# Two graph-attention layers and an FFN: layer 2's attention terms moved into the last head of layer 1, and three smaller moves

## The chip, the cores and the metric

The kernel runs on one core of a Trainium2 chip. The metric is device time in microseconds (us) of one execution. The engines named below are PE (TensorE, matrix products), DVE (VectorE), ACT (ScalarE), POOL (GpSimd) and SP (SyncE, which here issues nearly all DMAs). [...]

## The reference, cut to what matters

x has 1250 rows (nodes) of 768 values. With 21,250 edges (src, dst), the program computes

```python
def gat_layer(x, W, att_src, att_dst, bias, src, dst, heads, out_ch):
    h = (x @ W.T).reshape(n, heads, out_ch)
    a_src, a_dst = einsum('nhc,hc->nh', h, att_src), einsum('nhc,hc->nh', h, att_dst)
    e = leaky_relu(a_src[src] + a_dst[dst], 0.2)
    ex = exp(e - segment_max(e, dst)[dst])
    alpha = ex / (segment_sum(ex, dst)[dst] + 1e-16)
    return segment_sum(alpha[:, :, None] * h[src], dst) + bias

g = relu(gat_layer(layernorm(x), W1, ..., heads=8, out_ch=128))   # layer 1: 1250 x 1024
x = x + gat_layer(g, W2, ..., heads=1, out_ch=768)                # layer 2
x = x + ffn(layernorm(x))     # 768 -> 384 -> 768 with gelu; the first 6 rows take routed experts
```

## The kernel before, in words

The 1250 nodes are cut into 10 blocks of 125. A first stage counts the edges between every source and every destination node with one-hot products (to about 168 us); the counts (`ct`) then turn the sparse softmax into dense matrices. All sums are in float32.

**Layer 1** is a loop over eight heads `h` and ten source blocks `s` (from L740). For each, `weights` (L577) makes a tile `pt` of 125 sources by 1250 destinations in three steps: DVE adds and takes a maximum (L581), ACT takes Exp (L584), DVE limits and multiplies by the counts (L585). Three such tiles exist at a time. PE then multiplies the tile with the head's features, ten products of 129 columns (L749), into four accumulators `acc`. When a head is complete, `finish_head` (L654) runs inside the next head's step 0: DVE makes reciprocals (L661, L664), ACT rescales (`on`, L671), PE transposes (`h1tp`, L674), and ACT writes layer 1's output `g` with bias and relu (L675).

Other work is placed in the same loop. `top_of_block` (L555, its instruction at L557) takes, for one head and one source-side block, the row maximum over the neighbours, on DVE; the 120 of them that lie ahead of layer 2 are spread over the steps by hand (`top_steps`, L647). `load_destination_rows` (L562) prepares a head's two destination rows; its helper `rows_to_dram` (L518) transposes on PE, copies on DVE (L523) and sends the rows through DRAM, from where SP loads them broadcast to all partitions. `fold_att2` (L688, after heads 3 and 4) folds layer 2's attention vectors into W2, giving `v2` (1024 by 2): products on PE (L696), copies to `v_row` on DVE (L702), small transposes, copy to `v2`. `h2_part` (L722) makes one of the 20 pieces of the first half of layer 2's features `h2` (8 PE records each, L726); five pieces go into each of heads 4 to 7.

**The seam.** After head 7, `finish_head` runs once more, and layer 2's two attention terms are formed: `a2p` (L779 to L785) multiplies `v2` with `g`, head by head, in four column spans of 375, 375, 250 and 250 nodes. The four spans sit in four groups of PE's columns (32 each). DVE copies the result to `a2_row` (L787); the row goes to DRAM (`as2_d`), comes back broadcast, and DVE takes layer 2's ten tops. Meanwhile PE makes the second half of `h2` (another 20 pieces). Then come layer 2's weights (`weights2`, L823), its products (L905), a layer norm, and the FFN (`ffn_block`, L948), which stores each block with `store_rows` (L119).

**What sets the order.** A scheduler (the tile framework) decides the order on each engine when the program is built; it works from the order in which the kernel records operations and from its own costs. An edit in one place can thus move instructions elsewhere. Buffers come from pools: for PE's results there are six banks for products (`ps_mm`) and two for transposes (`ps_tr`).

Of the kernel before, what the change touches and what calls it, by code (L numbers as in the profile page):

```python
# [34 lines left out]
N = 1250  # L35
D = 768
E = 21250
H1, C1 = 8, 128
# [4 lines left out]
B = 125  # L43
NB = N // B
# [23 lines left out]
def gnn_ffn(  # L68
# [25 lines left out]
    nc = tc.nc  # L94
# [12 lines left out]
    def ps_mm(name):  # L107
        return mm_pool[0].tile([128, 512], F32, tag="mm", name=name)
# [266 lines left out]
    def act_copy(o, i):  # L375
        nc.scalar.activation(o, i, AF.Copy)  # L376
# [54 lines left out]
    groups, h1v = [], []  # L431
# [20 lines left out]
    for g in range(2):  # L452
        for h in range(H1):
            j = h % 4
            nc.tensor.matmul(
                vt[g][32 * j : 32 * j + 32, :384], att[:, h], w1n[h // 4][:, h % 4, g * 384 : (g + 1) * 384],
                start=(h < 4), stop=(h >= 4),
# [9 lines left out]
    p = ps_tr("vp")  # L467
    for k in range(KD):
        nc.tensor.matmul(
            p[:, 32 * k : 32 * k + 32], vt_s[:, k * 128 : (k + 1) * 128], pick_head,  # L470
            start=True, stop=True,
# [14 lines left out]
    spans = [(0, 3), (3, 6), (6, 8), (8, 10)]  # L486
    p = ps_mm("a1p")
# [30 lines left out]
    def rows_to_dram(cols, n, name, sp):  # L518

        p = ps_tr(f"{name}_p")  # L520
        nc.tensor.transpose(p[:n, :B], cols, ident[:B, :B])
        s = sp.tile([2 * NB, B], F32, tag="rowst", bufs=2, name=f"{name}_s")
        nc.vector.tensor_copy(s[:n], p[:n, :B])  # L523
        d = dram.tile([n, B], F32, name=f"{name}_d")
        nc.sync.dma_start(d, s[:n])
        return d
# [127 lines left out]
    def finish_head(h, acc):  # L654

        rec = ap.tile([B, NB], F32, tag="rec", bufs=2, name=f"rec{h}")
        avs = []
        for g in range(NG):
            n = min(PER, NB - g * PER)
            avs.append(acc[g][:B, : n * (C1 + 1)].rearrange("p (j c) -> p j c", j=n))  # L660
            nc.vector.tensor_scalar(  # L661
                rec[:, g * PER : g * PER + n], avs[g][:, :, C1], DEN_EPS, None, op0=OP.add
            )
        nc.vector.reciprocal(rec, rec)  # L664
        for g in range(NG):
            n = min(PER, NB - g * PER)
            av = avs[g]
            on = ap.tile([B, PER, C1], F32, tag="on", bufs=3, name=f"on{h}_{g}")
            for j in range(n):
                d = g * PER + j  # L670
                nc.scalar.activation(on[:, j], av[:, j, :C1], AF.Copy, scale=rec[:, d : d + 1])  # L671
            p = ps_tr(f"h1tp{h}_{g}")
            for j in range(n):
                nc.tensor.transpose(p[:, j * B : (j + 1) * B], on[:, j], ident[:B, :B])  # L674
            nc.scalar.activation(  # L675
                groups[h // 4][:, h % 4, g * PER * B : (g * PER + n) * B], p[:, : n * B],
                AF.Relu, bias=b1c[:, h : h + 1], scale=1.0,
            )
# [9 lines left out]
    def fold_att2(g):  # L688
        w2n = half_w(1, f"w2n{g}").rearrange("p (k f) -> p k f", k=KD)
        nc.sync.dma_start(  # L690
            w2n, w2[:, g * 512 : (g + 1) * 512].rearrange("(k p) f -> p k f", p=128)
        )
        p = ps_tr(f"v2p{g}")
        for k in range(KD):
            for j in range(2):
                nc.tensor.matmul(  # L696
                    p[32 * j : 32 * j + 2, :256], att2c[:, k], w2n[:, k, j * 256 : (j + 1) * 256],
                    start=(k == 0), stop=(k == KD - 1),
                )
        for j in range(2):  # L700
            c = g * 512 + j * 256
            nc.vector.tensor_copy(v2_row[:, c : c + 256], p[32 * j : 32 * j + 2, :256])  # L702
        p = ps_tr(f"v2tp{g}")
        for h in range(4 * g, 4 * g + 4):
            nc.tensor.transpose(
                p[:, 2 * h : 2 * h + 2], v2_row[:, h * C1 : (h + 1) * C1], ident[:2, :2]
            )
        nc.vector.tensor_copy(
            v2[:, 4 * g : 4 * g + 4],
            p[:, 8 * g : 8 * g + 8].rearrange("p (h t) -> p h t", h=4),  # L710
        )
# [10 lines left out]
    def h2_part(i, b, g):  # L722

        p = ps_mm(f"h2p{i}_{b}_{g}")
        for h in range(4):
            nc.tensor.matmul(  # L726
                p[:B, :384], groups[i][:, h, b * B : (b + 1) * B],
                w2h[i][:, h, g * 384 : (g + 1) * 384], start=(h == 0), stop=(h == 3),
            )
        o = h2[0][:, b, g * 384 : (g + 1) * 384]  # L730
        if i == 0:
            act_copy(o, p[:B, :384])
        else:
            nc.vector.tensor_add(o, p[:B, :384], o)

    h2_first = [(b, g) for b in range(NB) for g in range(2)]
    load_w2(0)
    todo = None
    for h in range(H1):
        hd = heads[h]  # L740
        acc = [ps_mm(f"acc{h}_{g}") for g in range(NG)]
        for s in range(NB):
            pt = ap.tile([B, N], F32, tag="pt", bufs=3, name=f"pt{h}_{s}")
            weights(pt, hd, as1_lo[:, h, s : s + 1], as1_hi[:, h, s : s + 1], s, 0, N)
            if s in top_steps.get(h, ()):
                tops.pop(0)()
            for d in range(NB):
                g, j = divmod(d, PER)
                nc.tensor.matmul(  # L749
                    acc[g][:B, j * (C1 + 1) : (j + 1) * (C1 + 1)],  # L750
                    pt[:, d * B : (d + 1) * B], h1v[h // 4][:, h % 4, s, :],
                    start=(s == 0 and j == 0), stop=(s == NB - 1), skip_group_check=True,
                )
            if s == 0 and todo is not None:
                finish_head(*todo)
            if s == 3 and h + 1 < H1:
                load_destination_rows(heads[h + 1], ap, a1[:, 1, h + 1], f"h{h + 1}", 2)
            if s == 0 and h == 3:
                load_source_row(heads[7], ap, as1_d[7], "h7")
            if h >= 4 and s in (2, 3, 5, 6, 8):  # L760
                h2_part(0, *h2_first.pop(0))
            if fill and s in (4, 7) and len(fill) > 2 * (3 - h) - (s == 7):
                fill.pop(0)()
        if h == 3:
            h2.append(big.tile([B, NB, D + 1], F32, tag="t", name="h2"))
            nc.gpsimd.memset(h2[0][:, :, D : D + 1], 1.0)
        if h in (3, 4):
            fold_att2(h - 3)
        if h == 5:
            load_w2(1)  # L770
        todo = h, acc
    finish_head(*todo)
    attn.close()


    second = ExitStack()
    sp = pool("second", stack=second)
    a2_row = sp.tile([2, N], F32, tag="src_row", bufs=1, name="a2_row")
    p = ps_mm("a2p")  # L779
    for h in range(H1):  # L780
        for j, (b0, b1) in enumerate(spans):
            nc.tensor.matmul(  # L782
                p[32 * j : 32 * j + 2, : (b1 - b0) * B], v2[:, h],
                groups[h // 4][:, h % 4, b0 * B : b1 * B], start=(h == 0), stop=(h == H1 - 1),
            )  # L785
    for j, (b0, b1) in enumerate(spans):
        nc.vector.tensor_copy(  # L787
            a2_row[:, b0 * B : b1 * B], p[32 * j : 32 * j + 2, : (b1 - b0) * B]
        )
    as2_d = dram.tile([1, N], F32, name="as2_d")  # L790
    nc.sync.dma_start(as2_d, a2_row[0:1])
    a2 = const.tile([B, NB, 2], F32, name="a2")
    p = ps_tr("a2tp")
# [154 lines left out]
    def ffn_block(q):  # L948

        gt = fp.tile([128, KH, 2, B], F32, tag="gt", bufs=2, name=f"gt{q}")  # L950
        for m in range(KH):
            p = ps_mm(f"f1_{q}_{m}")
            for k in range(KD):
                nc.tensor.matmul(  # L954
                    p[:, : 2 * B], wf1[:, k, m * 128 : (m + 1) * 128],
                    xt2[q][:, k].rearrange("p i j -> p (i j)"), start=(k == 0), stop=(k == KD - 1),
                )
            nc.scalar.activation(
                gt[:, m].rearrange("p i j -> p (i j)"), p[:, : 2 * B], AF.Gelu,
                bias=fc1c[:, m : m + 1], scale=1.0,  # L960
            )
        for i in range(2):
            d = 2 * q + i
            o = fp.tile([B, D], F32, tag="o", bufs=3, name=f"o{d}")
            nc.gpsimd.tensor_add(o, x2[d], fc2br)
            for g in range(2):
                p = ps_mm(f"f2_{d}_{g}")
                c = slice(g * 384, (g + 1) * 384)
                for m in range(KH):
                    nc.tensor.matmul(  # L970
                        p[:B, :384], gt[:, m, i, :], wf2[:, m, c],
                        start=(m == 0), stop=(m == KH - 1),
                    )
                nc.vector.tensor_add(o[:, c], p[:B, :384], o[:, c])  # L974

            r0 = NCLS if d == 0 else 0
            if d == 0:
                nc.sync.dma_start(out[r0:B], o[r0:])
            else:
                store_rows(out[d * B : (d + 1) * B], o)  # L980


# [161 lines left out]
```

## Time and profile before

| what | value |
|---|---|
| time, median of 3 runs | 787.17 us (786.72 to 787.53) |
| the profiled execution's own time | 786.1 us |
| its span, first to last instruction | 784.3 us |
| granted PE clock, mean | 0.991 of full speed |
| PE busy | 745.2 us (95%), 4612 instructions |
| DVE busy | 580.0 us (74%), 974 instructions |
| ACT busy | 323.7 us (41%), 589 instructions |
| POOL busy | 121.1 us (15%) |

Busy shares are means over stages with different limits. PE's ends are modelled from a pipeline, so that a busy PE can also be a PE that waits a little between two products; where exactness matters, starts of instructions are compared. In a row of instructions "x20" means 20 records; a float32 product of this kernel shows as two records, a transpose as one. The stages lie at: edge counts to 168 us, heads 0 to 3 from 200 to 338, heads 4 to 7 to 491, the seam to 503, the second half of `h2` to 553, layer 2 to 685, FFN to 784.

### The profile page before, as it was taken

The numbers are of one execution on the slowest core, as the hardware profiler recorded it, in microseconds if no ns is written. First come the engines' busy times: TensorE is split into PE (matmuls) and PEld (weight loads), VectorE is DVE, ScalarE is ACT, GpSimd is POOL, SyncE is SP. The second block draws the span as 40 slices with busy tenths as digits, with TensorE's granted clock in tenths as the row PEclk, the third lists the DMA queues.
The fourth block names the chain that finished last, engine by engine and source line by source line (L and its number), as shares of the span: only waits on it lengthen the run. The fifth ranks groups of instructions, "written<-read, shape, count | busy, mean of one in ns | idle before, by whom it ended". The sixth has DMA issues, their size and how long they took to land.

```text
span 784.3 us, 11527 instructions
## 1 busy us (share of the span) xinstructions
PE 745.2 (95%) x4612; PEld 493.4 (63%) x4612; DVE 580.0 (74%) x974; ACT 323.7 (41%) x589; POOL 121.1 (15%) x104
## 2 busy tenths in 40 slices
PE   4988998999989999899999999999999999999997
PEld 1553443544777777788888888455555555576755
DVE  7859999999999999999878785297856622251412
ACT  4989987522355546453635462202331300011000
POOL 5236677200000000000000000100010101023010
PEclk9999999899999999999999999999999999999999
DMA  9651000017002020422220100402211001094811
GB/s 238 217 207 41 3 1 1 2 67 242 37 2 67 1 67 1 147 81 67 81 67 1 67 1 2 152 0 69 64 36 31 29 20 40 0 316 111 329 40 40
DMA packets 21553, 58.49 MB, mean 75 GB/s; under 512 B 2385, under 2 KB 7627, under 8 KB 20344
## 3 DMA queue, kind: packets, MB, share of 16 engines
q1 hardware_dynamic: 21496, 57.72, 22.3%
q8 instruction: 37, 0.61, 0.3%
q14 instruction: 20, 0.16, 0.1%
HBM read 53.74 MB, written 3.98 MB: 74 GB/s over the span
## 4 chain that ended last, share of the span: by engine, by line
PE 60%; DVE 13%; issue 3%; ACT 2%; ACTq 0%; DVEq 0%
PE acc L905 15%; PE h2p L726 13%; PE acc L749 12%; DVE pt L581 6%; PE f L970 5%; PE f L954 5%; DVE pt L585 5%; PE h1p L443 4%; DVE unused L557 2%; PE h1tp L674 1%; ACT on L671 1%; PE a2p L782 1%; PE xt2p L372 1%; PE candp L1067 1%; PE v2p L696 1%
## 5 line engine op out<-in xcount | busy, mean ns | idle before, releaser
L584 ACT ACTIVATE pt<-pt,as_lo 125x1250 f32<-125x1250 f32 (+1 forms) x130 | 128.0, 1012 | 202.7 <-DVE pt L581 188.1
L749 PEld LDWEIGHTS acc<-g,pt 125*125 125x125 f32 x1600 | 185.0, 188 | 25.3 <-DVE pt L585 17.5
L749 PE MATMUL acc<-g,pt 125*125 125x129 f32 x1600 | 191.8, 275 | 7.1 <-DVE pt L585 7.1
L585 DVE SCALAR_TENSOR_TENSOR pt<-pt,ct 125x1250 f32<-125x1250 f32 (+1 forms) x130 | 133.2, 1053 | 11.9 <-ACT pt L584 11.5
L905 PE MATMUL acc<-h,pt 125*125 125x385 f32 (+1 forms) x400 | 129.7, 486 | 0.0
L581 DVE SCALAR_TENSOR_TENSOR pt<-rows_h,as_hi 125x1250 f32<-125x1250 f32 x80 | 119.8, 1514 | 11.0 <-PE acc L749 10.8
L443 PE MATMUL h1p<-w1s,xt 128*125 128x512 f32 x240 | 109.2, 597 | 0.6 <-ACT g L376 0.5
L905 PEld LDWEIGHTS acc<-h,pt 125*125 125x125 f32 x400 | 74.6, 187 | 53.9
L726 PE MATMUL h2p<-w2s,g 128*125 128x384 f32 x320 | 107.4, 487 | 0.0
L268 POOL TENSOR_SCALAR to<-node,dst_f 125x64 bf16<-125x64 f16 (+4 forms) x63 | 80.1, 1471 | 50.7 <-PE count L294 48.7
L726 PEld LDWEIGHTS h2p<-w2s,g 128*125 128x125 f32 x320 | 58.1, 187 | 37.7 <-issue 0.9
L294 PE MATMUL count<-ring,to 125*32 125x512 bf16 (+1 forms) x729 | 69.6, 362 | 6.4 <-DVE ring L219 5.3
L443 PEld LDWEIGHTS h1p<-w1s,xt 128*125 128x125 f32 x240 | 42.7, 188 | 47.4 <-issue 45.6
L294 PEld LDWEIGHTS <-to 125*32 125x32 bf16 x1068 | 37.7, 99 | 53.6 <-issue 23.8
L901 POOL TENSOR_TENSOR xb<-xb,b2r 125x768 f32<-125x768 f32 x10 | 18.5, 1850 | 326.0 <-DVE a_row L787 180.4
L219 DVE TENSOR_SCALAR ring<-node,src_f 125x1250 bf16<-125x1250 f16 x116 | 59.7, 545 | 7.0 <-PE count L294 4.5
L294 PE MATMUL count<-absent,to 125*32 125x512 bf16 (+1 forms) x339 | 52.4, 361 | 8.8 <-POOL to L268 6.6
L557 DVE CUSTOM_DVE_ANT_0 unused<-rows,absent 125x1250 bf16<-125x1250 f32 x40 | 58.0, 1449 | 0.4 <-DVEq L622 0.3
L557 DVE CUSTOM_DVE_ANT_0 unused<-srow_h,absent 125x1250 bf16<-125x1250 f32 x40 | 58.1, 1452 | 0.2
L974 DVE TENSOR_TENSOR o<-f,o 125x384 f32<-125x384 f32 x20 | 11.1, 557 | 52.5 <-PE f L970 27.4
L970 PE MATMUL f<-wf,gt 128*125 128x384 f32 x120 | 39.5, 486 | 0.0
L276 ACT ACTIVATE to<-away,ones 125x64 bf16<-125x64 f16 (+4 forms) x97 | 33.9, 349 | 13.3 <-PE count L294 9.4
(176 smaller groups left out, 619.5 us busy)
## 6 DMA issues: line engine op xcount, KB each, us to landing
rows_h<-r_h_d SPq DMA_DIRECT2D x8, 1250.0 KB
w_more<-in_atom_in_t SPq DMA_DIRECT2D x3, 1152.0 KB
w_more<-in_atom_out_t SPq DMA_DIRECT2D x3, 1152.0 KB
x<-in_x SPq DMA_DIRECT2D x10, 336.0 KB
xb<-in_x SPq DMA_DIRECT2D x10, 336.0 KB
srow_h<-as_d SPq DMA_DIRECT2D x5, 625.0 KB
w1n<-in_w SPq DMA_DIRECT2D x2, 1536.0 KB
w1s<-in_w1t SPq DMA_DIRECT2D x2, 1536.0 KB
```

Source lines behind the costliest of these rows:

```text
L219: return nc.vector.tensor_scalar(t, nodes, col, None, op0=OP.is_equal)
L268: eng.tensor_scalar(to[:, :w], node[:, n0 : n0 + w], dst_f[:, c : c + 1], None, op0=OP.is_equal)
L294: newest["count"] = nc.tensor.matmul(p[QUART * j : QUART * (j + 1), c0:c1], to[:, o : o + QUART], of[:, c0:c1], start=first, stop=last,)
L443: nc.tensor.matmul(p[:B], xt[:, k, b * B : (b + 1) * B], w1s[g][:, k], start=(k == 0), stop=(k == KD - 1),)
L557: nc.vector.tensor_tensor_reduce(out=unused, in0=hd.src_row, in1=absent[:, b], scale=1.0, scalar=-ABSENT, op0=OP.subtract, op1=OP.max, acc ...
L581: nc.vector.scalar_tensor_tensor(o, hd.rows[:, 0, c0:c1], hi, hd.rows[:, 1, c0:c1], op0=OP.add, op1=OP.max)
L584: nc.scalar.activation(o, o, AF.Exp, bias=lo, scale=1.0)
L585: nc.vector.scalar_tensor_tensor(o, o, 1.0, ct[:, s, c0:c1], op0=OP.min, op1=OP.mult)
L726: nc.tensor.matmul(p[:B, :384], groups[i][:, h, b * B : (b + 1) * B], w2h[i][:, h, g * 384 : (g + 1) * 384], start=(h == 0), stop=(h == 3),)
L749: nc.tensor.matmul(acc[g][:B, j * (C1 + 1) : (j + 1) * (C1 + 1)], pt[:, d * B : (d + 1) * B], h1v[h // 4][:, h % 4, s, :], start=(s == 0 a ...
L905: nc.tensor.matmul(acc[g][:B, : c1 - c0], pt[:, s, i * B : (i + 1) * B], h2[:, s, c0:c1], start=(s == 0), stop=(s == NB - 1),)
L970: nc.tensor.matmul(p[:B, :384], gt[:, m, i, :], wf2[:, m, c], start=(m == 0), stop=(m == KH - 1),)
```

## The change

Five things are edited.

1. `rows_to_dram` copies from PE's bank on ACT in place of DVE.
2. `fold_att2` takes four column quarters of 128 in four column groups in place of two halves of 256 in two, and its copies to `v_row` go to ACT.
3. Layer 2's attention terms use four nearly equal spans (312 or 313 nodes). A new function `attention2` forms them: heads 0 to 6 at step 6 of head 7, head 7 alone after its `finish_head`. ACT and DVE share the copies to `a2_row`.
4. Head 7 takes three pieces of `h2` in place of five. The two that are left are recorded at the seam, one before and one after the last `finish_head`.
5. The last output block is stored in column halves, each as soon as it is summed; its first 112 rows go by SP's queue, the last 13 by ACT's.

The diff, cut to its core:

```diff
@@ rows_to_dram
-        nc.vector.tensor_copy(s[:n], p[:n, :B])
+        act_copy(s[:n], p[:n, :B])
@@ fold_att2
-            for j in range(2):
+            for j in range(4):
                 nc.tensor.matmul(
-                    p[32 * j : 32 * j + 2, :256], att2c[:, k], w2n[:, k, j * 256 : (j + 1) * 256],
+                    p[32 * j : 32 * j + 2, :128], att2c[:, k], w2n[:, k, j * 128 : (j + 1) * 128],
                     start=(k == 0), stop=(k == KD - 1),
                 )
-        for j in range(2):
-            c = g * 512 + j * 256
-            nc.vector.tensor_copy(v2_row[:, c : c + 256], p[32 * j : 32 * j + 2, :256])
+        for j in range(4):
+            c = g * 512 + j * 128
+            act_copy(v2_row[:, c : c + 128], p[32 * j : 32 * j + 2, :128])
@@ new
+    spans2 = [(N * j // 4, N * (j + 1) // 4) for j in range(4)]
+    a2p = []
+
+    def attention2(hs):
+        if not a2p:
+            a2p.append(ps_mm("a2p"))
+        for h in hs:
+            for j, (n0, n1) in enumerate(spans2):
+                nc.tensor.matmul(
+                    a2p[0][32 * j : 32 * j + 2, : n1 - n0], v2[:, h],
+                    groups[h // 4][:, h % 4, n0:n1], start=(h == 0), stop=(h == H1 - 1),
+                )
@@ the loop over heads
-            if h >= 4 and s in (2, 3, 5, 6, 8):
+            if h >= 4 and s in ((2, 3, 5, 6, 8) if h < H1 - 1 else (2, 5, 8)):
                 h2_part(0, *h2_first.pop(0))
+            if h == H1 - 1 and s == 6:
+                attention2(range(H1 - 1))
@@ the seam
+    h2_part(0, *h2_first.pop(0))
     finish_head(*todo)
+    h2_part(0, *h2_first.pop(0))
+    attention2([H1 - 1])
     attn.close()
...
-    for j, (b0, b1) in enumerate(spans):
-        nc.vector.tensor_copy(
-            a2_row[:, b0 * B : b1 * B], p[32 * j : 32 * j + 2, : (b1 - b0) * B]
-        )
+    for j, (n0, n1) in enumerate(spans2):
+        eng = (act_copy, nc.vector.tensor_copy)[j % 2]
+        eng(a2_row[:, n0:n1], a2p[0][32 * j : 32 * j + 2, : n1 - n0])
@@ ffn_block
                 nc.vector.tensor_add(o[:, c], p[:B, :384], o[:, c])
+                if d == NB - 1:
+                    r0 = d * B
+                    nc.sync.dma_start(out[r0 : r0 + 112, c], o[:112, c])
+                    nc.scalar.dma_start(out[r0 + 112 : r0 + B, c], o[112:, c])
...
-            else:
+            elif d < NB - 1:
                 store_rows(out[d * B : (d + 1) * B], o)
```

## The prediction

> **What bounds the kernel now.** I read the profile in four steps: busy tenths, windows by stage, instructions in order of time, end. The tenths give the map: VectorE (DVE) is full up to about 345 us, TensorE (PE) from there on.
>
> ```profile
> PE   4988998999989999899999999999999999999997
> DVE  7859999999999999999878785297856622251412
> ```
>
> A digit stands for 19.6 us. PE looks full in the DVE stretch as well, but its ends are modelled, so the windows by head decide (us, then each engine's busy time: PE, its weight loads, DVE, ACT, POOL):
>
> ```profile
> 200.70:236.50 35.80, 33.30 (x257) 29.13 (x256) 35.68 (x36) 16.73 (x24) 0.00 (x0) 1.00 0.05 19
> 236.50:272.50 36.00, 34.70 (x238) 27.68 (x237) 35.77 (x40) 18.61 (x28) 0.00 (x0) 1.00 0.11 36
> 272.50:308.50 36.00, 34.70 (x237) 27.67 (x237) 35.90 (x40) 18.60 (x28) 0.00 (x0) 1.00 0.12 37
> 308.50:345.00 36.50, 34.45 (x261) 27.94 (x260) 36.08 (x41) 20.79 (x29) 0.12 (x1) 1.00 0.36 123
> 345.00:384.00 39.00, 39.00 (x271) 31.18 (x270) 37.26 (x45) 19.19 (x30) 0.00 (x0) 1.00 0.22 72
> 459.40:491.00 31.60, 31.60 (x210) 26.07 (x209) 20.24 (x17) 12.82 (x17) 0.00 (x0) 1.00 0.03 5
> 491.00:503.50 12.50, 12.50 (x92) 5.02 (x91) 2.35 (x7) 4.55 (x14) 1.57 (x1) 1.00 0.53 178
> ```
>
> In heads 0 to 3 (first four rows) DVE lacks 0.1 to 0.4 us of the whole: every microsecond on its queue there lengthens the kernel. From head 4 on PE has no gap and DVE has; there only PE's work counts. The granted clock is 1.00 in all rows. DVE's prices, from its instructions in order of time (start, duration):
>
> ```profile
> 241.37 0.27 DVE L523 COPY r_h_s<-r_h_p 20x125 f32<-20x125 f32 x1
> 241.57 1.50 DVE L581 SCALAR_TENSOR_TENSOR pt<-rows_h,as_hi 125x1250 f32<-125x1250 f32 x1
> ...
> 243.15 1.44 DVE L557 CUSTOM_DVE_ANT_0 unused<-srow_h,absent 125x1250 bf16<-125x1250 f32 x1
> 244.53 0.07 DVE L557 DVE_READ_ACCUMULATOR2_ANT top<- 125x1 f32 x1
> 244.53 1.46 DVE L585 SCALAR_TENSOR_TENSOR pt<-pt,ct 125x1250 f32<-125x1250 f32 x1
> ```
>
> From start to start: a row maximum ("top", L557) 1.38, the copy L523 0.20. The seam behind head 7, on PE:
>
> ```profile
> 491.01 1.42 PE L782 MATMUL a2p<-g,v 128*2 128x375 f32 x10
> 492.37 0.80 PE L674 MATMUL h1tp<-ident,on 125*128 125x125 f32 x4
> 493.10 0.79 PE L782 MATMUL a2p<-g,v 128*2 128x375 f32 x6
> 493.82 0.33 PE L674 MATMUL h1tp<-ident,on 125*128 125x125 f32 x1
> 494.08 0.79 PE L782 MATMUL a2p<-g,v 128*2 128x375 f32 x2
> ...
> 497.26 2.68 PE L782 MATMUL a2p<-g,v 128*2 128x375 f32 x30
> 499.88 1.55 PE L726 MATMUL h2p<-w2s,g 128*125 128x384 f32 x4
> ```
>
> Two a2p records between transposes hold PE for 0.72 us (494.08 to 494.80), as long as eight do at 495.05. So the interleaving is itself dear.
>
> **1. What the new order does to DVE (a loss).** The scheduler places the work anew, because three small copies change engine. I counted in the two built programs the tops that stand on DVE before given tiles: before head 4's first weight tile 114 of 120 now and 119 then; before its third 114 and 120. In the kernel now the last six run inside head 4, where PE sets the pace; in the new order all six stand in DVE's own stretch: 6 x 1.38 = 8.3. Taken off that stretch: the r-row copy, now on ACT, five times 0.20 = 1.0; v_row's two copies of the first fold (338.34 to 339.13) 0.8. Left: 6.5. DVE's waits for ACT in this stretch (0.23, 0.18, 0.26) and 0.17 ahead of v_row are filled by the denser order: 5.6. Ends: 4.6, if PE's first product of h2 (2.58, now placed ahead of head 4's third tile) covers most of the last top; 6.5, if no wait goes. On ACT (busy 16.7 of 36 us a head) the copies are free; each r copy stands behind one Exp there, and the broadcast row it feeds is wanted some 15 us later. If that cover failed, the next head's first tile would be late by the copy's delay, about 1.3 (one Exp).
>
> **2. The fold of att2 in quarters, on ACT.** The second fold lies where PE sets the pace: 375.58 to 378.26, 2.68 for 24 records. It becomes 48 records of 128 columns in four column groups. The nearest row is L1029, 128 columns in three groups: first to last start 722.7 to 724.0 for 36 records, 0.036 each; 48 x 0.036 = 1.7, a gain of 1.0. [...] I take the row, since its records are the same size, and keep 0.2 as the end. The first fold lies in DVE's stretch: PE's saving is worth nothing there. Its load (1.5 MB) is issued when the last h1 product is done (321.35 now) and is off the wire six microseconds later; in the new order the fold stands one tile earlier, three tiles (2.2 to 2.8 us each, some seven in all) behind that issue. A late load would hold PE, then DVE at the copy of v, one for one. At head 5's start PE now takes 5.25 us (378.26 to 383.51) for 30 records at 0.11 and 10 transposes at 0.106, 4.4 together; of the 0.85 lost I take back 0.4 (ends 0 and 0.85), since the four ACT copies stand ahead of the head's rescaling.
>
> **3. The seam.** Now: 491.01 to 499.88, 8.87; then a2tp and six h2 records to 503.46, 3.58, less 6 x 0.3225: 1.64. Together 10.5 us that are no h2 product. Then: seven heads of a2p in one run inside head 7, 56 records. By the run of 30 above (0.087 each) scaled 313/375, 4.1; by L1023 (four equal groups of 384 columns, 48 records in 4.01) scaled 313/384, 3.8; if the mean span rules instead of the widest, 4.9. I take 4.0. At the seam one head 0.6, ten transposes 1.1, 0.3 of waits, a2tp 1.6: 7.5 in all, a gain of 3.0; with 3.8 and no waits 3.4, with 4.9 and 1 us of waits 1.4. I take 2.8. What hides the waits: two h2 products (2.58 each) moved from head 7 to either side of the rescaling chain, which now takes from 491.31 to about 498 under the a2p. PE's sum of h2 is unchanged. a2p holds one of six banks from tile 6 on, acc four, so the last three h2 products share the sixth; each needs its ACT copy (0.47) first, and two tiles or six transposes lie between.
>
> SP's queue: the first FFN weight load (1.15 MB) waits for the last h2 product, so it moves from 488.91 to within 2 us of the row as2_d and its broadcast. It is moved past b2's row and one block of x; as2_d moves ahead of the next two pieces of x. Queued behind both is the broadcast, for which layer 2's tops wait. Now the tops start at 510.05, the first layer-2 weights end about 548 and PE wants them at 553.34: 5 us of slack, of which such a load takes 3 (at the 373 to 402 GB/s that the transfers of 491 to 493 reach). No cost; beyond 5 it is late one for one. POOL's order is unchanged.
>
> **4. Last block in halves.** The end now:
>
> ```profile
> 779.75 0.56 DVE L974 TENSOR_TENSOR o<-f,o 125x384 f32<-125x384 f32 x1 [1.32 <-PE f L970]
> ...
> 780.37 0.32 SPq L121 DMA_DIRECT2D out<-o  x1
> 780.74 0.38 SPq L122 DMA_DIRECT2D out<-o  x1
> ```
>
> The windows of the transfer show 384 KB from 781.05 to 782.5, and the span ends at 784.3. With half of it sent earlier, 0.7 goes[...]. [...] I take the row; 0.4 and 1.0 (the second issue's 0.37 gone too) are the ends.
>
> **Sum.** 5.6 - 1.0 - 0.4 - 2.8 - 0.7 = +0.7 us. The profiled execution: 784.3 span and 1.8 around it, 786.1, to 786.8; it lies 1.1 under the median of 787.17, which becomes 787.9. The ends add up to -1.7 (4.6 - 1.0 - 0.85 - 3.4 - 1.0) and +4.5 (6.5 - 0.2 - 0 - 1.4 - 0.4).
>
> **Rivals.** *Faster:* two of the six extra tops cost nothing: the one ahead of head 0, where PE is in h1 products until 200.73, and the last one, under head 4's h2 product. Then 0.7 - 2 x 1.38 = -2.1: 785.1. For it: PE's queue really has that product there. Against: DVE waits only 0.12 for PE at 202.97, so at the start there is no room. It decides when the loss of step 1 falls under 3.3. *Slower:* the loads. If the first fold's weights land 2 us after PE reaches them, DVE stands at the copy of v: 789.9. For it: six against seven microseconds is thin. Against: the load was never late, and DVE's own queue is slower than my count if anything. It decides from 1 us of lateness on. A kin of it, the quarters bringing nothing (fold 0.2, seam 1.4), gives 790.1. *The regrouping does not reach the seam:* PE's gain is given back because layer 2's first tops are late; beyond the 5 us of slack, 788 to 791.
>
> **How the numbers follow.** Within 0.2% (1.6 us, about what a measurement of this kernel can tell from no change) is the likeliest, 0.51: gain and loss nearly cancel. Slower cases together 0.30, faster 0.19. The range leaves half of the faster case's chance and a third of the slower ones' out: 785.0 to 790.1; the likeliest case's own is 786 to 788.7.
>
> **What would show it.** Head 4's first acc product some 5 to 6 us later than 338.23, with at most one top on DVE after it; head 4 to 5 shorter by 1 to 1.5; a2p of seven heads in about 4 us; from head 7's last acc to layer 2's first about 60.5 (22 products of 2.58 and 3.7), against 62.3 now with 20 products; the last store's tail under 3.5 us after DVE's last add. Wrong if DVE shows gaps in heads 0 to 3, if PE waits on w2n, or if layer 2's acc starts behind a wait.

## The result, and the profile after

| | time, median | executions | mean granted clock of these |
|---|---|---|---|
| before | 787.35 us | 786.72 to 787.76 (4) | 0.991 in the trace |
| changed | 791.51 us | 788.2, 791.14, 791.89, 792.83 | 0.989, 0.985, 0.985, 0.983 |

The changed kernel is slower: 1.0044 times the time before, 95% interval 1.0028 to 1.006. I had said 787.9 with a range to 790.1; 791.5 lies above it. The traced execution of the changed kernel is the quickest of its four: 788.2 us, span 786.4, against 786.1 and 784.3 before. So the trace shows 2.1 of the 4.2 us. The rest must be looked for in the column of clocks: the more time, the lower the clock.

Of the changed kernel, first the windows of heads 0 to 3 (us, then busy time of PE, its weight loads, DVE, ACT, POOL; then the granted clock):

```profile
200.00:236.00 36.00, 31.27 (x223) 26.81 (x222) 35.72 (x36) 13.24 (x11) 0.00 (x0) 0.96 0.05 18
236.00:272.00 36.00, 34.69 (x238) 28.21 (x238) 35.94 (x39) 17.62 (x26) 0.00 (x0) 0.99 0.11 37
272.00:308.00 36.00, 33.04 (x226) 26.59 (x225) 35.94 (x42) 18.96 (x27) 0.00 (x0) 1.00 0.11 37
308.00:345.00 37.00, 33.14 (x290) 28.78 (x289) 36.79 (x40) 20.46 (x31) 0.11 (x1) 1.00 0.35 121
```

DVE is as full as before; PE is busy 31.3 to 34.7 us where it was busy 33.3 to 34.7; and the first two rows have a clock below 1.00, which no row of these heads had before. Instructions of PE in order of time, then 2 us windows at the same place:

```profile
224.55 4.67 PE L764 MATMUL acc<-g,pt 125*125 125x129 f32 x40 [2.32 <-DVE pt L585]
231.53 5.45 PE L764 MATMUL acc<-g,pt 125*125 125x129 f32 x32 [2.32 <-DVE pt L585]
```

```profile
232.00:234.00 2.00, 2.00 (x17) 2.00 (x16) 2.00 (x3) 0.00 (x0) 0.00 (x0) 0.75 0.00 0
234.00:236.00 2.00, 2.00 (x11) 2.00 (x11) 1.72 (x5) 1.34 (x1) 0.00 (x0) 0.50 0.00 0
236.00:238.00 2.00, 1.05 (x8) 0.85 (x7) 1.98 (x4) 1.46 (x2) 0.00 (x0) 0.89 0.00 0
```

PE stands 2.32 us for a tile (the bracket gives the wait and who ended it), starts again, and from 233.0 on runs at half clock: 32 records take 5.45 us where 40 took 4.67. The missing clock adds up to 2 x (0.25 + 0.50 + 0.11) = 1.72 us, or 3.4 us at half speed. The page's row of clock in tenths shows 9 in this slice, as it does nearly everywhere, and hides the fall.

What makes such a gap can be read at the turn from head 1 to head 2. DVE of the changed kernel does two tops in a row, five short operations and two L581 before it finishes a tile with L585:

```profile
267.64 1.45 DVE L557 CUSTOM_DVE_ANT_0 unused<-srow_h,absent 125x1250 bf16<-125x1250 f32 x1
...
269.13 1.46 DVE L557 CUSTOM_DVE_ANT_0 unused<-srow_h,absent 125x1250 bf16<-125x1250 f32 x1
...
270.66 1.51 DVE L581 SCALAR_TENSOR_TENSOR pt<-rows_h,as_hi 125x1250 f32<-125x1250 f32 x1
...
272.22 1.51 DVE L581 SCALAR_TENSOR_TENSOR pt<-rows_h,as_hi 125x1250 f32<-125x1250 f32 x1
...
273.78 2.88 DVE L585 SCALAR_TENSOR_TENSOR pt<-pt,ct 125x1250 f32<-125x1250 f32 x2
```

The L585 ahead of these starts at 266.2, so two L585 lie 7.6 us apart. The kernel before has as many tops and L581 between two L585 there, 7.4 us apart:

```profile
267.19 1.45 DVE L585 SCALAR_TENSOR_TENSOR pt<-pt,ct 125x1250 f32<-125x1250 f32 x1
...
274.59 2.83 DVE L585 SCALAR_TENSOR_TENSOR pt<-pt,ct 125x1250 f32<-125x1250 f32 x2
```

So DVE's order alone is not the gap. PE's order differs too (before, then changed):

```profile
273.31 3.60 PE L443 MATMUL h1p<-w1s,xt 128*125 128x512 f32 x8
276.75 4.57 PE L749 MATMUL acc<-g,pt 125*125 125x129 f32 x40
```

```profile
261.59 5.32 PE L443 MATMUL h1p<-w1s,xt 128*125 128x512 f32 x12
266.74 5.89 PE L764 MATMUL acc<-g,pt 125*125 125x129 f32 x52
275.23 0.48 PE L764 MATMUL acc<-g,pt 125*125 125x129 f32 x2 [2.60 <-DVE pt L585]
```

Before, eight records of h1 (the features of heads 4 to 7) and, ahead of them, the ten transposes of the finished head fill PE's time. In the new order twelve records of h1 stand ahead of the finished tiles, and the reciprocals that the transposes need come only behind the two tops. The finished tiles then last PE 5.9 us, and it stands 2.60. (At 224 and 231 us it is DVE's order: it finishes tiles two at a time, 7.0 us apart, and two tiles last PE 4.7.) The changed kernel has such gaps of 2.15 to 2.60 us at four or five places, by the execution, in heads 0 to 3; the longest of before there is 1.49:

```profile
228.31 2.46 PE L749 MATMUL acc<-g,pt 125*125 125x129 f32 x20 [1.49 <-DVE pt L585]
```

The parts that were to gain did so. PE around the second fold, at the seam, and the end:

```profile
382.31 1.49 PE L696 MATMUL v2p<-w2n,att2c 128*2 128x128 f32 x48
383.73 1.81 PE L764 MATMUL acc<-g,pt 125*125 125x129 f32 x14
```

```profile
482.33 3.87 PE L746 MATMUL a2p<-g,v 128*2 128x312 f32 x56
...
502.00 0.71 PE L746 MATMUL a2p<-g,v 128*2 128x312 f32 x8
...
556.38 8.89 PE L917 MATMUL acc<-h,pt 125*125 125x385 f32 x27
```

```profile
781.43 2.20 SPq L989 DMA_DIRECT2D out<-o  x2
781.43 2.24 ACTq L990 DMA_DIRECT2D out<-o  x2
782.72 0.56 DVE L986 TENSOR_TENSOR o<-f,o 125x384 f32<-125x384 f32 x1 [1.32 <-PE f L982]
```

The shift against before at some marks, in us:

| mark | before | changed | shift |
|---|---|---|---|
| DVE, first L581 of head 0 | 191.6 | 193.7 | +2.1 |
| DVE, first L581 of head 4 | 330.8 | 336.7 | +5.9 |
| PE, second fold begins | 375.58 | 382.31 | +6.7 |
| PE, acc behind it | 378.26 | 383.73 | +5.5 |
| PE, layer 2's first acc | 553.34 | 556.38 | +3.0 |
| DVE, last add | 779.75 | 782.72 | +3.0 |
| span's end | 784.3 | 786.4 | +2.1 |

### The profile page after: what moved, and what is told of

Same layout as the page of the kernel before. It is cut to its first block, busy times and chain, and to the rows that moved or that the text cites. A ratio compares the mean times of both kernels' runs of the same rounds, so it can differ in the third digit from the quotient of the medians.

```text
span 786.4 us, 11630 instructions
## 1 busy us (share of the span) xinstructions
PE 741.1 (94%) x4660; PEld 495.2 (63%) x4660; DVE 577.3 (73%) x959; ACT 328.7 (42%) x608; POOL 121.5 (15%) x104
## 4 chain that ended last, share of the span: by engine, by line
PE 54%; DVE 21%; issue 3%; ACT 1%; DVEq 0%; ACTq 0%
PE acc L917 15%; PE h2p L726 13%; PE acc L764 11%; DVE pt L581 8%; DVE unused L557 6%; DVE pt L585 6%; PE f L982 5%; PE f L966 5%; PE h1tp L674 1%; PE xt2p L372 1%; PE candp L1083 1%; PE a2p L746 1%; PE hidp L1039 1%; ACT pt L584 0%; DVE rec L661 0%
## 5 line engine op out<-in xcount | busy, mean ns | idle before, releaser
L585 DVE SCALAR_TENSOR_TENSOR pt<-pt,ct 125x1250 f32<-125x1250 f32 (+1 forms) x130 | 133.7, 1052 | 12.9 <-ACT pt L584 12.4
L581 DVE SCALAR_TENSOR_TENSOR pt<-rows_h,as_hi 125x1250 f32<-125x1250 f32 x80 | 120.3, 1517 | 13.6 <-PE acc L764 13.6
```

The lines of the kernel that those rows point to most:

```text
L581: nc.vector.scalar_tensor_tensor(o, hd.rows[:, 0, c0:c1], hi, hd.rows[:, 1, c0:c1], op0=OP.add, op1=OP.max)
L585: nc.vector.scalar_tensor_tensor(o, o, 1.0, ct[:, s, c0:c1], op0=OP.min, op1=OP.mult)
```

## The experiments

Three theories. **1:** the moved tops are the loss, and PE's longer gaps let the clock fall, in some executions more often than in others. **2:** the order alone; the clock has no part. **3:** the loss comes from the seam's side (loads, banks, layer 2's start). All runs of one group share a chip and the runs of the kernel before, whose medians were 787.09 (first four), 787.35 (next four), 787.71 (next four) and 787.25 (last three).

**The rows copy alone, and all but it.** First the kernel before with one line changed:

```diff
@@ rows_to_dram
-        nc.vector.tensor_copy(s[:n], p[:n, :B])
+        act_copy(s[:n], p[:n, :B])
```

> The kernel before with one edit: rows_to_dram copies on ACT. The built order then has the tops where the changed kernel has them: all but one ahead of head 4's first weight tile. Theory 1 (the moved tops are the loss, and longer PE gaps in heads 0 to 3 let the clock fall in some executions): head 4 starts 5 to 7 us later than before, time 791.5 to 794.5, the executions of one kernel further apart than before's 1.1 us, with the slower ones at a lower mean clock. Theory 2 (the order alone, the clock has no part): 792 to 793.5, spread as before. Theory 3 (the loss comes from the seam's side: loads, banks, layer 2's start): this edit does not touch it, so 786.5 to 787.5.

Measured: 798.19 (797.03 to 798.99), clock 0.980 to 0.985; 1.0138 times before, 1.0122 to 1.0154. Slower still than expected. Then the changed kernel with this line put back:

> The changed kernel with the one copy of rows_to_dram back on DVE. The built order then has the tops of before inside head 4. Theories 1 and 2: head 4 starts within 1 us of before's 338.23, and the gains of the fold (1.3), seam (1.1) and store (0.9) are left: 783.5 to 784.5. Theory 3: the loss stays, 790 to 792.

Measured: 784.63 (782.56 to 784.91), 0.9967 (0.9956 to 0.9978). So the loss hangs on this one line, and theory 3 falls. In the first of the two kernels the clock fell behind all four gaps over 2 us in heads 0 to 3 (once for two periods of 3.4 us), 8.5 us of clock in all, and DVE, which hardly ever waited there before, waits for PE. Its waits from 190 to 345 us, kernel before and then this one (total, times, longest):

```profile
DVE pt L585 <- ACT pt L584: 0.5, 2, 0.3
```

```profile
DVE pt L581 <- PE acc L749: 5.1, 9, 1.2
```

The path is the tile buffers: there are three, and L581 can't write one until PE has read it. A PE at half speed gives it back late (in the changed kernel 32 acc records took 5.45 us where the clock fell, 40 took 4.67 where it held). That accounts for this run: head 4 starts 11.2 later on DVE, of which 2.0 are there at head 0, four tops in heads 0 to 3 make 5.5, the copies saved 0.8, and the waits 4.6; together 11.3. No wait for a head's broadcast rows is in either list, so the copy's move to ACT did not make the rows late.

**Tops held.** If the tops' place is the loss, they can be ordered behind their own step:

```diff
@@ weights
-        nc.vector.scalar_tensor_tensor(o, o, 1.0, ct[:, s, c0:c1], op0=OP.min, op1=OP.mult)
+        newest["w"] = nc.vector.scalar_tensor_tensor(o, o, 1.0, ct[:, s, c0:c1], op0=OP.min, op1=OP.mult)
@@ the loop over heads
-                tops.pop(0)()
+                with tc.issue_after(newest["w"].ins):
+                    tops.pop(0)()
```

> The changed kernel, and each of the 30 tops recorded in the loop is ordered behind its own step's L585 on DVE, so that none moves forward: 14 stay in heads 0 to 3, 6 in head 4, 7 in head 5, 3 in head 6. Theories 1 and 2: ten tops fewer than before in the DVE-paced stretch, at most about 6 us of it to be had because PE is busy 33.3 to 34.7 of each head's 36 us; head 5 with 7 tops comes near DVE's limit and gives some 2 back. 778 to 782. Theory 3: 789 to 791.

Measured: 787.6 (785.27 to 789.75), 1.0012 (1.0004 to 1.002).

> As the run with the tops held, with other steps: 18 in heads 0 to 3 (5, 5, 4, 4), 5 in head 4, 5 in head 5, 2 in head 6, every other step. PE paces heads 4 to 7 throughout. Heads 0 to 3 need DVE about 36.0 - 1.5 x 1.38 = 34 us each, about what PE needs: 777 to 780, and less than with the tops merely held. If the clock has a part, its mean is at least before's 0.991.

Measured: 788.01 (785.99 to 790.27), 1.0011 (1.0003 to 1.0019). And later, with the steps moved away from the heads' ends:

> As the runs with the tops held, with steps that keep tops away from the turn of a head: steps 2, 3, 5, 6 in heads 0 to 3, 2, 3, 5, 6, 7, 8 in head 4, 1, 2, 4, 5, 6, 7 in head 5, 1, 2 in head 6. In both earlier runs a top stood on DVE just ahead of a new head's first L585, PE stood 1.6 to 3.2 us there, and the clock fell behind it. Theory 1: no PE gap over 1.5 us in heads 0 to 4, no clock below 1.00 from 200 to 490 us, 778 to 782. If a gap is not what lets the clock fall, the time stays at 786 to 788 as with the other steps.

Measured: 789.69 (788.54 to 793.14), 1.0037 (1.0025 to 1.0049). All three lie above their expectations, by 5.6, 8.0 and 7.7 us from the upper ends. The trace of the last one shows why, DVE first, then PE:

```profile
192.67 4.38 DVE L581 SCALAR_TENSOR_TENSOR pt<-rows_h,as_hi 125x1250 f32<-125x1250 f32 x3 [8.58 <-DMA rows_h<-r_h_d]
```

```profile
226.02 8.53 PE L765 MATMUL acc<-g,pt 125*125 125x129 f32 x60 [3.41 <-DVE pt L585]
```

DVE waits 8.6 us for head 0's rows to come back. In the kernel before six of these tops fill that time at no cost; held, they cost it again. From there to 345 us DVE waits another 10.7 us, in 13 waits, for PE: with fewer tops in heads 0 to 3 PE has become the bound there. The second row is a gap of 3.41 us, with the clock falling behind it (60 records in 8.53): three L581 in a row behind a top starve PE as well as two tops do. In the first held run a fall lay on the turn to head 4, where PE paces: 3.4 us of clock gone and DVE waiting 2.8 and 1.5 us for PE behind it. So holding tops said nothing against theory 1, but it did not undo the move either.

**Gaps filled.** A direct test of the clock: keep DVE's order to the instruction, and give PE work in the gaps whose results nobody uses. First on the kernel with the rows copy alone:

```diff
@@ the loop over heads, after acc's products
+            if (h, s) in ((1, 9), (2, 9)):
+                pf = ps_mm(f"fill{h}_{s}")
+                for i in range(8):
+                    nc.tensor.matmul(
+                        pf[:B, :60], pt[:, :B], pt[:, 384 : 384 + 60],
+                        start=(i == 0), stop=(i == 7),
+                    )
```

> The kernel of the first run (before with rows_to_dram on ACT), with eight idle products of 60 columns added on PE behind the last tile of head 1 and of head 2, about 1.0 to 1.8 us each; their sums are used nowhere. DVE's order is the same to the instruction; PE's has only these products more. In the first run PE stood 2.6 us at both places and the clock fell to a half right behind both (at 276 and at 314). Theory 1: the gaps shrink to under 1.6 us, no clock below 1.00 behind these two places, and the time falls by 3 to 5 us against the first run: 793 to 795.5. Theory 2 (the order alone): PE has more work and DVE the same: 798 to 799, and the clock as in the first run.

Measured: 797.63 (797.32 to 797.91), 1.0123 (1.0105 to 1.0142): about as without. Yet the clock no longer fell behind either place. This filler has a fault: it reads the tile, so DVE waited for it (0.73 us at each place), in this trace the first fold's weights came 0.97 us after PE wanted them, and a fall came at 350 us, where PE paces. By its clock it speaks for theory 1, by its time against it; it settles nothing. So once more on the changed kernel, with a filler that reads a constant and holds no tile, beside the unfilled kernel on the same chip:

> The changed kernel once more, unaltered, beside its filled twin on the same chip. 790.5 to 792, single executions from about 788 to 793, the higher ones at a lower mean clock (788.2 at 0.989, 791.1 and 791.9 at 0.985, 792.8 at 0.983 so far).

```diff
@@ the loop over heads, after acc's products
+            if (h, s) in ((1, 9), (2, 9)):
+                pf = ps_mm(f"fill{h}_{s}")
+                for i in range(14):
+                    nc.tensor.matmul(
+                        pf[:B, :60], ident[:, :B], ident[:, :60],
+                        start=(i == 0), stop=(i == 13),
+                    )
```

> The changed kernel with 14 idle products of 60 columns on PE behind the last tile of head 1 and of head 2, about 1.6 us each by the first filled run's 0.058 a record; they read a constant, so DVE waits for none of them; their sums are used nowhere. DVE's order is the same to the instruction. PE's gaps there shrink from 2.6 to about 1. If the falling clock behind these gaps costs time: no clock below 1.00 behind them, and 1 to 3 us under the unfilled twin: 788.5 to 790.5. If DVE's order alone sets the time: equal to the twin within 0.5.

Measured: unfilled 792.44, single executions 788.43 and 788.88 at a clock of 0.989, six from 790.94 to 794.7 at 0.981 to 0.984; 1.0056 times before (1.0037 to 1.0075). Filled 789.23, all 22 executions from 788.02 to 790.71, clock 0.985 or more; 1.0019 (1.0012 to 1.0025). More work on PE, the same order on DVE, and 3.2 us less. PE of the filled kernel at the place of the 2.60 gap:

```profile
267.81 3.79 PE L764 MATMUL acc<-g,pt 125*125 125x129 f32 x33
271.44 3.16 PE L772 MATMUL fill<-ident 128*125 128x60 f32 x28
274.44 1.76 PE L764 MATMUL acc<-g,pt 125*125 125x129 f32 x14
```

No gap is left here (the filler takes 3.0 us, twice what I had expected: 0.107 a record). Three gaps of 2.16 to 2.32 us remain earlier, at 225, 232 and 238 us, without a fall in this trace: the clock stays at 1.00 from 200 to 360 us. Here is the stretch in which it falls in the last trace below:

```profile
276.00:278.00 2.00, 2.00 (x20) 2.00 (x20) 2.00 (x2) 2.00 (x8) 0.00 (x0) 1.00 0.00 0
278.00:280.00 2.00, 2.00 (x20) 1.95 (x20) 2.00 (x4) 1.99 (x6) 0.00 (x0) 1.00 0.00 0
```

Theory 2 falls: with DVE's order kept, PE's gaps alone were worth 3.2 us.

**Two more traces of the changed kernel** (its third and fourth), since both earlier ones were of quick executions:

> The changed kernel, one execution with its trace. So far its traces were of executions at a mean clock of 0.989, with one fall of the clock in heads 0 to 3. If this one is at 0.981 to 0.985: two or more falls of 3.4 us or more at half clock behind PE gaps of 2.1 to 2.6 us in heads 0 to 3, DVE waiting for PE behind them, 790.9 to 794.7. If the falls lie elsewhere (edge counts), my account of the spread is wrong.

> As the run before: another execution of the changed kernel with its trace.

Measured: 793.39 (span 790.3, clock 0.984) and 790.7 (span 788.9, clock 0.982). In the fourth trace the clock fell at three gaps. The last of these falls, in 2 us windows, and PE there:

```profile
276.00:278.00 2.00, 1.35 (x6) 1.35 (x7) 1.98 (x3) 2.00 (x8) 0.00 (x0) 0.58 0.00 0
278.00:280.00 2.00, 2.00 (x13) 2.00 (x12) 1.49 (x4) 0.90 (x4) 0.00 (x0) 0.57 0.00 0
```

```profile
276.65 0.80 PE L764 MATMUL acc<-g,pt 125*125 125x129 f32 x2 [2.60 <-DVE pt L585]
...
278.09 1.84 PE L764 MATMUL acc<-g,pt 125*125 125x129 f32 x8
```

Eight records take 1.84 us here and 1.26 at the same place of the first trace, where the clock holds. DVE's waits for PE from 190 to 345 us, in this trace and in the filled kernel's:

```profile
DVE pt L581 <- PE acc L764: 2.9, 5, 1.0
```

```profile
DVE rec L661 <- PE acc L764: 0.2, 1, 0.2
```

Set side by side, with the span counted from head 0's first L581 to leave the edge counts out:

| kernel, trace | clock lost in heads 0 to 4, us | DVE's waits for PE, 190 to 345 us | span from head 0 on, us |
|---|---|---|---|
| before | 0 | none listed | 592.7 |
| changed, filled | 0 | 0.2 | 592.3 |
| changed, first | 1.7 | 0.4 | 592.7 |
| changed, second (the run again) | 1.7 | 1.1 | 593.4 |
| changed, third | 3.4 | 2.4 | 594.9 |
| changed, fourth | 5.1 | 2.9 | 595.7 |

One, one, two and three falls (1.7 us of clock each) go with 0.4, 1.1, 2.6 and 3.4 us more than the filled kernel, and DVE's waits for PE grow in step. That is about 1.1 us a fall. The rest of the spread lies elsewhere: head 0 begins at 195.4 in the third trace and at 193.2 in the fourth, though both lose 8.5 us of clock in the edge counts, so the clock does not explain this part. And in the third trace the execution's time is 3.1 above its span, where most have 1.8. Neither is explained: of the 5.2 us by which this execution is slower than the first, only 2.2 lie behind head 0's start.

**Single parts.** The seam alone (item 3 and 4 of the change), the last block's halves alone (item 5), the fold alone (item 2), each as in the change's diff:

> The kernel before with the seam's part alone: four equal spans, seven heads' share in head 7, two h2 pieces kept for the seam, copies to a2_row shared. The orders of heads 0 to 6 stay as before. My sum said 2.8 less; the profile of the changed kernel read 1.2 less between head 7's last acc and layer 2's first, with two more h2 pieces in it and a2p's 3.8 us moved into head 7. Theories 1 and 2: 785.0 to 786.5 (a gain of 0.8 to 2.0). Theory 3 (the seam brings the loss): 789 to 792.

Measured: 783.75 (783.56 to 786.31), 0.9956 (0.9939 to 0.9973): 3.6 less by the medians, more than expected. From head 0 on 589.9, which is 2.8 less.

> The kernel before with the last block stored in halves alone. My sum said 0.7 less (0.4 to 1.0); the changed kernel's tail read 0.9 less. All theories: 786.0 to 786.6.

Measured: 785.95 (785.17 to 787.65), 0.9981 (0.9974 to 0.9987): 1.4 less by the medians; from head 0 on 591.8, 0.9 less.

> The kernel before with the fold's part alone (quarters in four groups, copies to v_row on ACT). The built order moves hardly a top (159 of 165 by head 4, as before). The changed kernel's trace read 1.26 less in the second fold. If that is the whole: 785.8 to 786.3. If ACT's copies cost at the turn of heads 4 and 5, as the changed kernel's 0.3 there hints: 786.2 to 787.

Measured: 787.14 (786.35 to 788.44), 0.9997 (0.9989 to 1.0005), no difference that can be told, and less of a gain than expected; from head 0 on 592.0, 0.7 less. Its trace has the fold 1.3 us shorter and part of that back at the next head's start, where PE waits for the copies on ACT:

```profile
376.98 1.49 PE L696 MATMUL v2p<-w2n,att2c 128*2 128x128 f32 x48
...
380.68 0.22 PE L705 MATMUL v2tp<-ident,v_row 2*128 2x2 f32 x1 [0.47 <-ACT v_row L376]
```

**The clear gains together**, and these with late tops:

> The two parts that were clear gains alone, and nothing else: the seam (3.6 less alone) and the last block in halves (1.4 less alone). DVE's order in heads 0 to 6 stays that of before. If they add up: 782 to 783, under both kernels and under the run without the rows copy (784.6).

Measured: 783.25 (782.85 to 784.46), 0.9942 (0.9929 to 0.9956): a little above the expectation and under both kernels. With the fold added (all but the rows copy) the gain on the kernel before was 2.5 us, here it is 4.5, while the traces from head 0 on differ by 0.3 (588.4 and 588.7); that is not explained.

> The run of seam and store with the ten tops of heads 5 and 6 in the order held behind their own step's L585, all others as the scheduler places them: 14 tops in heads 0 to 3 ahead of head 4's first tile (18 in the kernel before), none in head 4. DVE's stretch loses 4 x 1.38 = 5.5, of which PE (idle 1.3 and 2.0 us in heads 2 and 3) can use about 2 to 3; no top stands ahead of a turn's first L585 in heads 0 to 4, so no gap over 1.5 us and no fall of the clock there: 780 to 781.5. If moving tops is useless in itself, as the held runs could suggest: 783 to 784.5.

Measured: 783.56 (781.58 to 783.83), 0.9945 (0.9932 to 0.9958): no gain over the run before, and the second of the two cases expected. DVE does reach head 4 2.7 us earlier, counted from head 0. No gap over 1.49 and no fall of the clock is left in heads 0 to 4, but DVE now waits for PE in head 3 (2.7 us in four waits): PE is the bound there. And a new wait of PE opened at the turn to head 6, 2.14 us for ACT's rescaling.

## Why the prediction was wrong

**Step 1, the size: right. Its cover: wrong.** Six tops were to cost 5.6 by the time PE leaves DVE's stretch. Where they went: one ahead of head 0, four in heads 0 to 3 (22 in the trace, 18 before), one in head 4. From head 0's first L581 to the second fold the changed kernel took 188.7 us in the first trace and 188.2 in the filled one, before 184.0: 4.2 to 4.7. The top ahead of head 0 should add 1.38. Over seven traces with the moved tops head 0 began at 193.9 in the mean, over seven with the order of before at 192.8: 1.1, under a scatter of up to 1.5 either way. Together 5.3 to 5.8.

The step that failed is the sentence that in heads 0 to 3 only DVE's microseconds count, and with it "the granted clock is 1.00 in all rows", taken as if it would stay so. The same rows have 1.3 to 2.5 us a head in which PE is idle; I put these at nothing and never asked in what pieces they would come. The new order, of DVE and of PE, bunches them into gaps of 2.15 to 2.60 us, the clock falls at some of them, and through the three tile buffers that reaches DVE. This term is missing from the sum: 3.2 us by the filled twin. My range did not hold it. The ends of my sum did reach 4.5 us over the kernel before (791.7), and the measured time lies inside them; but they stand for other costs that did not come, so that would have been luck. One of my signs of being wrong, DVE with gaps in heads 0 to 3, came true: up to 2.9 us of waits for PE. A warning was there: the same trace of before has the clock falling in the edge counts, behind waits of PE for DVE:

```profile
134.73 0.71 PE L294 MATMUL count<-ring,to 125*32 125x512 bf16 x10 [1.51 <-DVE ring L219]
136.64 0.59 PE L294 MATMUL count<-ring,to 125*32 125x512 bf16 x1 [1.21 <-DVE ring L219]
```

```profile
134.00:136.00 2.00, 0.71 (x10) 0.23 (x10) 2.00 (x6) 0.00 (x0) 1.26 (x2) 1.00 0.00 0
136.00:138.00 2.00, 0.59 (x1) 0.10 (x1) 2.00 (x6) 0.00 (x0) 0.70 (x1) 0.59 0.00 0
138.00:140.00 2.00, 1.52 (x17) 0.68 (x20) 2.00 (x5) 0.00 (x0) 0.00 (x0) 0.50 0.00 0
```

**Step 2.** The fold gained 1.26, not 1.0: 48 records of 128 columns in 1.42 us, 0.030 each, where the row that I took has 0.036. The lower end of 0.2, which also stands in the upper end of the sum and in the rival at 790.1, was my estimate and not taken from any trace; the fold of 2.5 us that goes with it (2.68 less 0.2) was not seen. At head 5's start the changed kernel lost 0.2 where I took back 0.4; the fold alone has PE waiting 0.47 us there for ACT's copies.

**Step 3.** I said 2.8; the seam alone measures 2.8 from head 0 on (3.6 by the medians), and in the changed kernel it takes the shift from +5.7 at head 7 to +3.0 at layer 2. (The terms said add up to 7.6, not 7.5, which changes little.) Seven heads of a2p took 3.8 us (4.0 said), the stretch from head 7's last acc (its end, 495.4) to layer 2 61.0 (60.5 said). The layer-2 tops and the moved load cost nothing.

**Step 4.** From the last add to the span's end 3.7 us, before 4.55: 0.9 (0.7 said; the sign "under 3.5" did not follow from 0.7, which leaves 3.85). My lower end of 0.4 was an estimate that no trace shows; the 384 KB that took 1.45 us before give 0.7 for the half.

**The sum.** +0.7 was said, and the filled twin, which keeps every step and lacks only the gaps behind heads 1 and 2, is 1.5 slower than before by its medians, 1.0019 times. So the likeliest case was right for a kernel whose clock holds in these heads, as it does in the filled twin's trace.

**The rivals.** Two tops at no cost: no, the loss to the second fold is whole. Whether one of them was free isn't shown; that head 0 began 1.1 later in the mean speaks against it for the top ahead of head 0. The late fold weights: no wait in the changed kernel's first trace, but 0.97 and 0.87 us in two other orders, so the thin margin was real. Late layer-2 tops: no. The rows copied on ACT were not late either. None of the three slower cases was the one that came.

## What to carry to other kernels

Idle time of an engine that is not the bound isn't free by its sum alone; ask how it is cut. In heads 0 to 7 here no gap of PE up to 1.49 us had a fall of the clock in it or behind it in the five traces counted below, and of the 14 over 2 us 6 had; where the clock fell, the engine that paces waited (DVE 2.9 us in the trace with three falls, 0.2 in the one with none). When a scheduler places the work anew, look not only at how many instructions move, but at what stands between two releases of the next engine's input and what that engine has to do meanwhile. Work moved into such gaps can pay though it is of no use. And undo the smallest edit first, since here one copy of 0.2 us decided the sign. Compare the traced execution's own time and clock with the others' before reading it: the best of four is not the kernel.

## What was unexpected of the hardware

The clock falls to 0.50 for about 3.4 us (1.70 to 1.72 us of clock in each single fall from 200 us on) or a multiple of that: 6.8 us at 338 us in the first held run, 10.2 us in the edge counts of the changed kernel's third trace. All waits of PE in heads 0 to 7 of five traces (the kernel before; the first, third and fourth of the changed kernel; the run of seam and store with late tops):

| PE's gap | gaps | with a fall in it or behind it |
|---|---|---|
| 2.14 to 2.60 us | 14 | 6 |
| 1.53 to 1.76 us | 4 | 0 |
| up to 1.49 us | all others | 0 |

In other traces a gap of 3.41 us had a fall behind it (tops away from the heads' ends, 226 us), and one of 1.70 had a fall in it (first held run, 338 us).

Why does the same gap of 2.60 us bring a fall in one execution and not in the next? In each of the 17 traces the clock changes, down or up, only at multiples of 3.413 us from one another (to within 0.03 us by the 2 us windows, edge counts included). In the kernel before, the clock holds for 34.13 and for 81.92 us between its falls in the edge counts, in the first trace of the changed kernel for 88.75 us ahead of the fall at 233.0: 10, 24 and 26 times 3.413. In the fourth trace of the changed kernel the falls begin at 225.1, 238.8 and 276.3, which are 4 and 11 such steps apart. Where these steps lie against the kernel differs from execution to execution: the fall in the edge counts begins at 137.4 us in the changed kernel's first trace, at 141.1 in the third and at 136.4 in the fourth. Cut at the steps, the 2.60 us gap looks like this, in the fourth trace and then in the first:

```profile
272.89:276.30 3.41, 1.16 (x11) 0.96 (x9) 3.41 (x6) 2.39 (x2) 0.00 (x0) 1.00 0.00 0
```

```profile
270.55:273.97 3.42, 2.08 (x19) 1.89 (x18) 3.42 (x10) 1.48 (x2) 0.00 (x0) 1.00 0.00 0
273.97:277.38 3.41, 2.15 (x17) 2.04 (x18) 3.39 (x3) 3.41 (x10) 0.00 (x0) 1.00 0.00 0
```

In the fourth, one step has 2.25 us of idle PE (3.41 less 1.16), and the next is at half clock. In the first, two steps share the gap with 1.34 and 1.26, and the clock holds. The gaps over 2 us in the three traces of the changed kernel, each with the longest part of it that lies within one step:

| trace | gap begins, us | gap, us | within one step, us | clock in the next step |
|---|---|---|---|---|
| third | 223.96 | 2.32 | 2.32 | 0.50 |
| fourth | 221.77 | 2.32 | 2.32 | 0.50 |
| third | 275.40 | 2.60 | 2.28 | 0.50 |
| fourth | 274.05 | 2.60 | 2.25 | 0.50 |
| fourth | 235.96 | 2.16 | 2.16 | 0.50 |
| first | 229.21 | 2.32 | 1.94 | 0.50 |
| first | 222.22 | 2.32 | 1.78 | 1.00 |
| first | 309.92 | 2.60 | 1.59 | 1.00 |
| third | 238.56 | 2.15 | 1.57 | 1.00 |
| third | 232.60 | 2.17 | 1.46 | 1.00 |
| third | 313.80 | 2.60 | 1.43 | 1.00 |
| fourth | 312.45 | 2.60 | 1.40 | 1.00 |
| first | 272.63 | 2.60 | 1.34 | 1.00 |

The ends of PE's products are modelled, so that the idle times are not exact. The fall of the first held run does not fit in: the step ahead of it, up to 338.16 us, has only 0.65 us of the gap of 1.70, and that is not explained. In the edge counts the step ahead of the fall near 137 has 2.4 us idle in the kernel before and 2.3 in the first trace of the changed kernel; in the kernel before it is made up of the waits of 1.2 to 1.5 shown above.
